# Sparse graph layers on one core: five summed slots in the last nine tiles, a new order of the last tiles, and three smaller edits

## The chip, the cores and the metric

The kernel runs on one core of one Trainium2 chip. The metric is the device time of one launch in microseconds; every number below is in microseconds unless it says otherwise. PE is TensorE, POOL is GpSimd, SP is SyncE, which here only issues DMAs.

## The reference, cut to what matters

Two layers on N = 4096 nodes with D = 512 features. `adj` is about 0.2% dense with a diagonal of its own, so a row has about nine entries.

```python
# layer 0
a = adj + eye;  d = sum(a, axis=1) ** -0.5
out = relu((d[:, None] * a * d[None, :]) @ x @ W.T + b)
x = layernorm(x + out)
# layer 1: attention over 8 heads, key size 64
q, k, v = x @ Wq[h], x @ Wk[h], x @ Wv[h]
scores = q @ k.T / 8 + 0.01 * eye - 1e16 * (1 - maximum(adj, eye))
out = sum over h of softmax(scores) @ v @ Wo[h]
x = layernorm(x + out)
```

Every stored edge is below one, so `1 - adj` times 1e16 sends all scores of a row but the largest to zero weight, and the largest is a node's own. Layer 1 then is `x @ sum_h(Wv[h] @ Wo[h])`. The kernel computes that, and proves on the chip that the inputs are of this kind; otherwise it runs a general version, which is not entered here.

## The kernel before

**First pass** (lines 1049-1091, `for t in range(NT + 1)`): 32 tiles of 128 rows of `adj`, 2 MB each, come in on SP. For each tile ScalarE sums the rows (`sum_rows`, L710) or adds up their negative parts (`sum_negative`, L715), POOL turns the sum into the degree's inverse root (`scaling`, L722-725), and VectorE finds the eight largest entries of each of eight segments and their places (`scan`, L752 and L753). Tiles are taken in the order `early + resident + again`: 14 early ones, 5 that stay in SBUF, and 13 that were read once already for their row sums and are read a second time later (`reload`, L994-998). Beside this the projection `u = x @ W.T` of every tile is formed on PE: `transpose_rows` (L689), a copy to SBUF on ScalarE (`evacuate`, L694), four fp32 matmuls against `wT` (`times`, L703). When the degree is known, `keep_y` (L736-738) scales it and POOL stores it to `y` in DRAM. The list `due` says at which t a tile's y is kept; `lo` and `hi` (L1058) say for which due times the projection is formed at step t: for t + 1 up to t = 24, for t + 1 and t + 2 at t = 25, for t + 2 after that. The accumulators `acc` have five PSUM buffers, `x_t` has six SBUF buffers.

**Sorting and matching.** `sorting` (L756-839) packs value and column into integer keys and takes the 24 largest of a row in three rounds of eight (`top8`), setting the taken ones to zero between rounds (`drop`, L785-788). `match` (L911) then moves edges of rows that have more than nine into free slots of other rows, so that each tile has KH = 9 slots of 128 edges. `cols_all` holds the columns (L896), `wr_all` the weights.

**Second pass** (lines 1280-1367, `for i in range(NT + 2)`, inner loop over k = 0..8). Tile i is `order[i]`. For each of its nine slots POOL gathers 128 rows of y (`gather`, L1110), one indirect DMA a slot, 18 slots ahead, into 19 buffers. PE multiplies each gathered 128x512 block by a 128x128 selection matrix (`spread`, built on ScalarE, L1007-1020) and accumulates in PSUM (L1316). Slots 0 to 4 (SAME = 5) share one matrix, so their rows may be scaled and summed first and multiplied once: `presum` (L1123-1131) scales slot 0 on ScalarE (L1127) and adds the others on VectorE (L1129). The list `summed` says how many slots of a tile are so summed:

```python
    summed = [1] + [2] * (NT - 3) + [SAME] * 2
```

That is one in tile 0, two in tiles 1 to 29, five in tiles 30 and 31, whose products `summed_products` (L1133-1140, L1137) issues with the summed one last. Then VectorE adds the own row (`scaled`, L1180) and the residual (`residual`, L1188); PE transposes (step "T") and multiplies by `wvo`, the product of the layer-1 weights (step "M"); ScalarE and VectorE form the two layernorms as one scaling (steps "Q", "V", L1207 and L1210), and `finish` (step "F", L1217-1220) scales into `r_t` and stores it through ScalarE's queue. The table in `at` says how many iterations behind, and at which k, each step of a tile is issued: `far` for tiles 0 to 29, `near` for the last two. Tile 31 is done in two halves of 256 columns. VectorE's scan and sorting of the later tiles run in between, in shares (`some`, L1327).

The order of instructions on an engine is set by a planner from its own costs; the source order is kept only where a call asks for it (`tc.keep_in_program_order`). Each engine takes its instructions in that order.

Of the kernel before, what the change touches and what calls it, by code (L numbers as in the profile page):

```python
# [419 lines left out]
def few_edges_below_one(  # L420
# [271 lines left out]
    def evacuate(pool, name, pt, pinned=False):  # L692
        dst = pool.tile([P, ND, P], FP, name=name, bufs=2)
        copy = nc.scalar.copy(dst.rearrange("p c s -> p (c s)"), pt[:, :D])  # L694
        if pinned:
            tc.keep_in_program_order(copy)
        return dst

    def times(srcT, w, u=None, dcs=range(ND)):
        if u is None:  # L700
            u = ps_a.tile([P, D], FP, name="acc")
        for dc in dcs:
            nc.tensor.matmul(  # L703
                u, srcT[:, dc, :], w[:, dc, :], start=(dc == 0), stop=(dc == ND - 1)
            )
        return u
# [49 lines left out]
    def sorting(t, idx, rec):  # L756
# [26 lines left out]
            return lambda: nc.vector.max(top[:, f, r * 8 : r * 8 + 8], keyf[:, f])  # L783

        def drop(f, r):  # L785
            return lambda: nc.vector.match_replace(
                keyf[:, f], top[:, f, r * 8 : r * 8 + 8], keyf[:, f], 0.0
            )

        short = [  # L790
            [
# [202 lines left out]
    def reload():  # L994

        t = queue.pop(0)
        reloaded.append(t)
        a_tiles[t] = load_a(t)

    def spread(t, s_t, k, alone=False):  # L1000

# [21 lines left out]
    xs, us = {}, {}  # L1023
    DEEP = 3
    RATE = 9
    EARLIER = NT - 7
    due = [(t + 1, t) for t in range(NT) if t not in early]
    for n, t in enumerate(early):
        at = max(t + 3, -(-STEPS * (n + 1) // RATE) + 1)
# [19 lines left out]
    for t in range(NT + 1):  # L1049
        if t == 0:  # L1050
            su1 = load_second_weights()
        if t + DEEP < NT:
            a_tiles[t + DEEP] = load_first(t + DEEP)
        if t == 3:
            order_second_weights()
            setup = second_weights(su1)

        lo, hi = t + 1 + (t > EARLIER), t + 1 + (t >= EARLIER)  # L1058
        ahead = [j for at, j in due if lo <= at <= hi]
        pts = []  # L1060
        for j in ahead:
            prefetch(1)
            pts.append(transpose_rows(xs.pop(j)))
        kind, begin, end = next(setup, (None,) * 3) if len(ahead) < 2 else (None,) * 3
        got = begin() if kind == "t" else None
        if t < NT:
            if t in early:
                sum_negative(t, a_tiles[t])
            else:
                sum_rows(deg_all[:, t : t + 1], a_tiles[t][:, : N // 2 if t == NT - 1 else N])  # L1070
                more = None
                if t == NT - 1:
                    more = small.tile([P, 1], FP, name="more")
                    sum_rows(more, a_tiles[t][:, N // 2 :])
                scaling(t, more)
            if t in again:
                del a_tiles[t]
        if left:
            left()
            left = None  # L1080
        for j in [j for at, j in due if at == t]:
            keep_y(j, us.pop(j))
        for j, pt in zip(ahead, pts):
            us[j] = times(evacuate(p1, "xT", pt, t >= EARLIER), wT)
        if kind == "t":
            end(got)
        if kind == "p":
            left = lambda end=end, pa=begin(): end(pa)
        if t < NT - 5:
            match(*ALL)  # L1090
        some((t + 1) * RATE)
# [6 lines left out]
    p2 = ctx.enter_context(tc.tile_pool(name="second", bufs=2))  # L1098
    AHEAD = 18

    SUMMED = (NT - 2, NT - 1)
    summed = [1] + [2] * (NT - 3) + [SAME] * 2
    slots = {}

    def gather(j):
# [24 lines left out]
            g, slots.pop(i * KH + k), w, g, op0=ALU.mult, op1=ALU.add  # L1130
        )

    def summed_products(i, pos, c=slice(0, D)):  # L1133

        k = SAME + pos if pos < KH - SAME else None
        g = slots[i * KH if k is None else i * KH + k]
        nc.tensor.matmul(  # L1137
            zs[i][:, c], mats[i][:, KH if k is None else k, :], g[:, c],
            start=False, stop=(k is None),
        )  # L1140

    def build(count):

# [27 lines left out]
    def bias(i, c=slice(0, D)):  # L1171

        nc.tensor.matmul(zs[i][:, c], ones3, b3[:, c], start=True, stop=False)
# [42 lines left out]

    def finish(i):  # L1217
        r_t = p2.tile([P, D], FP, name="r_t")
        nc.scalar.activation(r_t, ws.pop(i), AF.Copy, scale=sts.pop(i)[:, 4:5])  # L1219
        nc.scalar.dma_start(out[ts(order[i], P), :], r_t)  # L1220

# [45 lines left out]

    def at(step, i, k):  # L1270

        near = {"T": (1, 5), "M": (1, 8), "Q": (2, 2), "V": (2, 3), "F": (2, 7)}
        far = {"T": (2, 0), "M": (2, 6), "Q": (3, 1), "V": (3, 4), "F": (3, 8)}
        for table, tiles in ((near, range(NT - 2, NT)), (far, range(NT - 2))):
            behind, place = table[step]
            if k == place and i - behind in tiles:
                return i - behind
        return None

    for i in range(NT + 2):  # L1280
# [6 lines left out]
        for k in range(KH):  # L1287
# [6 lines left out]
                ws[t] = times(hTs.pop(t), wvo)  # L1294
            if i == NT - 1:

                if k <= KH - SAME:
                    summed_products(i, k, HALVES[0])
                if k == 6:
                    scaled(i, HALVES[0])  # L1300
                    residual(i, HALVES[0])
                if k == 7:
                    pts[i] = transpose_rows(hs[i], (0, 1))
                if k == 8:
                    bias(i, HALVES[1])
                    for n in range(KH - SAME + 1):
                        summed_products(i, n, HALVES[1])
                    hTs[i] = p2.tile([P, ND, P], FP, name="hT", bufs=2)
                    nc.scalar.copy(
                        hTs[i][:, 0:2].rearrange("p c s -> p (c s)"), pts[i][:, : 2 * P]  # L1310
                    )
            elif i in SUMMED:
                if k <= KH - SAME:
                    summed_products(i, k)
            elif i < NT and not 0 < k < summed[i]:
                nc.tensor.matmul(  # L1316
                    zs[i], mats[i][:, KH if k < summed[i] > 1 else k, :], slots.pop(i * KH + k),
                    start=False, stop=(k == KH - 1),
                )
# [13 lines left out]
                ws[p] = times(hTs[p], wvo, dcs=(0, 1))  # L1333
            if ends and k == 2:
                pts[p] = transpose_rows(hs[p], (2, 3))
                nc.scalar.copy(hTs[p][:, 2:].rearrange("p c s -> p (c s)"), pts[p][:, 2 * P : D])
                nc.vector.tensor_tensor(sts[p][:, 0:1], sts[p][:, 0:1], sts[p][:, 4:5], ALU.add)
            if ends and k == 3:
                times(hTs[p], wvo, ws[p], (2, 3))
# [59 lines left out]
```

## Time and profile before

| what | us |
|---|---|
| median of 3 runs (lowest, highest) | 646.42 (645.92, 649.11) |
| profiled execution, time | 646.95 |
| profiled execution, span of the core | 645.2 |
| busy PE / VectorE / ScalarE / POOL | 545.8 / 546.0 / 504.6 / 352.8 |
| mean granted clock of PE | 0.946 of full speed |
| bytes moved by DMA | 217.68 MB, mean 337 GB/s |

The time of the profiled execution holds 1.75 beyond the span. A matmul of fp32 operands shows as two records. An idle time is put down to what came last before the instruction started. The profile's line numbers are those of the kernel before.

### The profile page before, as it was taken

What the parts mean: (1) busy time and instruction counts of PE and PEld (TensorE: products, weight loads), DVE (VectorE), ACT (ScalarE), POOL (GpSimd) and SP (SyncE); (2) the same over time, 40 slices, a digit from 0 to 9 for tenths busy, and PEclk for the clock granted to TensorE, in tenths of its full rate; (3) what the DMA queues carried; (4) which work ended last, traced back from release to release, by engine and by line L of the source; (5) the groups of instructions that cost most, each with busy time, mean ns of one, the idle gap of its engine ahead of it and who ended that gap; (6) DMA issues with size and microseconds to landing.
All of it is one profiled execution on the core that took longest, in us unless ns stands there. A gap on an engine that the chain in (4) does not pass through costs nothing. (4 is left out here: it accounts for less than half of the span.)

```text
span 645.2 us, 7918 instructions
## 1 busy us (share of the span) xinstructions
PE 545.8 (85%) x1579; PEld 251.2 (39%) x1579; DVE 546.0 (85%) x2143; ACT 504.6 (78%) x1114; POOL 352.8 (55%) x465
## 2 busy tenths in 40 slices
PE   1699876488979756799898898999999999999993
PEld 1354332233434222344343343444444444444352
DVE  5699999999999995998899999999999995431521
ACT  1868667786988957699989877889988998986543
POOL 5222223223342377676776767767677777777700
PEclk9899987788979968799899998999999999999998
DMA  9999999799999388999999999999998888888721
GB/s 331 402 421 421 424 428 423 286 422 424 423 425 419 157 270 284 400 351 385 387 408 409 401 401 387 305 348 348 328 362 280 269 263 300 281 285 276 238 70 54
DMA packets 51515, 217.68 MB, mean 337 GB/s; under 512 B 8062, under 2 KB 9086, under 8 KB 45441
## 3 DMA queue, kind: packets, MB, share of 16 engines
q1 hardware_dynamic: 18128, 115.35, 44.7%
q0 software_dynamic: 28192, 92.30, 41.0%
q10 hardware_dynamic: 5136, 9.44, 3.9%
q14 instruction: 45, 0.36, 0.2%
q8 instruction: 14, 0.23, 0.1%
HBM read 200.28 MB, written 16.78 MB: 336 GB/s over the span
## 5 line engine op out<-in xcount | busy, mean ns | idle before, releaser
L1110 POOL DMA_INDIRECT g<-y,cols_all x288 | 282.5, 981 | 107.1 <-issue 43.1
L1316 PE MATMUL acc<-g,s_t 128*128 128x512 f32 x482 | 232.0, 618 | 28.0 <-DVE g L1129 17.1
L752 DVE MAX8 v_all<-a_t 128x8 f32<-128x512 f32 x256 | 166.3, 677 | 8.2 <-DMA a_t<-in_adj_dram 8.2
L753 DVE FIND_INDEX8 idx<-v_all,a_t 128x8 uint32<-128x512 f32 x256 | 173.0, 683 | 0.0
L703 PE MATMUL acc<-wT,xT 128*128 128x512 f32 x256 | 128.9, 658 | 31.4 <-ACT xT L694 31.3
L1316 PEld LDWEIGHTS acc<-g,s_t 128*128 128x128 f32 x482 | 89.8, 196 | 125.9 <-issue 95.1
L703 PE MATMUL acc<-wvo,hT 128*128 128x512 f32 x256 | 117.6, 601 | 4.5 <-ACT hT L694 3.8
L715 ACT ACTIVATE dump<-a_t 128x2048 uint8<-128x2048 f32 (+1 forms) x50 | 119.1, 2382 | 0.0
L703 PEld LDWEIGHTS acc<-wT,xT 128*128 128x128 f32 x256 | 52.1, 211 | 95.6 <-issue 59.1
L703 PEld LDWEIGHTS acc<-wvo,hT 128*128 128x128 f32 x256 | 48.6, 192 | 65.1 <-issue 57.0
L1007 ACT ACTIVATE sq<-cols,wr_all 128x128 f32<-128x128 f32 x160 | 58.7, 394 | 0.2
L1011 ACT ACTIVATE s_t<-sq,wr_all 128x128 f32<-128x128 f32 x128 | 58.2, 486 | 0.7 <-ACT sq L1007 0.2
L722 POOL TENSOR_SCALAR deg<-deg_all 128x1 f32<-128x1 f32 x32 | 7.1, 224 | 83.3 <-DVE deg_all L971 48.8
L1129 DVE SCALAR_TENSOR_TENSOR g<-g,wr_all 128x512 f32<-128x512 f32 x37 | 27.5, 743 | 25.5 <-ACT g L1127 22.7
L710 ACT ACTIVATE dump<-a_n 128x4096 uint8<-128x4096 f32 x13 | 47.3, 3636 | 0.0
L550 POOL DMA_DIRECT2D x_t<-in_x_dram x32 | 18.0, 566 | 46.3 <-PE pt L689 37.6
L1127 ACT ACTIVATE g<-g,wr_all 128x512 f32<-128x512 f32 x31 | 22.1, 713 | 24.0 <-DMA g<-y,cols_all 16.8
L783 DVE MAX8 top<-key 128x8 f32<-128x64 f32 x192 | 36.0, 213 | 0.3
L1180 DVE SCALAR_TENSOR_TENSOR h<-yo,own_all,acc 128x512 f32<-128x512 f32 (+1 forms) x33 | 23.8, 720 | 11.2 <-PE acc L1316 7.8
L1020 ACT ACTIVATE s_t<-s_t,wr_all 128x128 f32<-128x128 f32 x92 | 33.0, 391 | 0.0
L694 ACT COPY hT<-pt 128x512 f32<-128x512 f32 x31 | 18.0, 579 | 16.4 <-PE pt L689 15.4
L694 ACT COPY xT<-pt 128x512 f32<-128x512 f32 x32 | 18.3, 594 | 11.5 <-PE pt L689 11.5
(134 smaller groups left out, 676.8 us busy)
## 6 DMA issues: line engine op xcount, KB each, us to landing
a_t<-in_adj_dram SPq DMA_DIRECT2D x30, 2048.0 KB, 15.3
a_n<-in_adj_dram SPq DMA_DIRECT2D x13, 2048.0 KB, 13.6
x_t<-in_x_dram POOLq DMA_DIRECT2D x32, 256.0 KB, 12.6
yo<-y SPq DMA_DIRECT2D x32, 256.0 KB, 6.6
x_t<-in_x_dram SPq DMA_DIRECT2D x32, 256.0 KB, 5.9
out_dram<-r_t ACTq DMA_DIRECT2D x32, 256.0 KB, 5.2
y<-y_t POOLq DMA_DIRECT2D x18, 256.0 KB, 13.6
g<-y,cols_all POOLq DMA_INDIRECT x288, 6.3
```

Of the source, the lines that this page charges most:

```text
L694: copy = nc.scalar.copy(dst.rearrange("p c s -> p (c s)"), pt[:, :D])
L703: nc.tensor.matmul(u, srcT[:, dc, :], w[:, dc, :], start=(dc == 0), stop=(dc == ND - 1))
L710: nc.scalar.activation(dump[:, : part.shape[1]], part, AF.Copy, accum_out=dst)
L715: nc.scalar.activation(dump[:, o], a_t[:, o], AF.Relu, scale=-1.0, accum_out=neg_all[:, t, halves[0] : halves[0] + 1],)
L752: long.append(lambda o=o, seg=seg: nc.vector.max(v[:, o], seg))
L753: long.append(lambda o=o, seg=seg: nc.vector.max_index(idx[:, o], v[:, o], seg))
L783: return lambda: nc.vector.max(top[:, f, r * 8 : r * 8 + 8], keyf[:, f])
L1007: nc.scalar.activation(sq, cols1, AF.Square, bias=wr[:, 2, k : k + 1])
L1011: nc.scalar.activation(s_t[:, k, :], away(), AF.Relu, scale=wr[:, 3, k : k + 1], bias=wr[:, 1, k : k + 1],)
L1020: nc.scalar.activation(s_t[:, k, :], s_t[:, KH, :], AF.Copy, scale=wr[:, 1, k : k + 1])
L1110: nc.gpsimd.indirect_dma_start(out=slots[j], out_offset=None, in_=y[:, :], in_offset=bass.IndirectOffsetOnAxis(ap=cols_all[:, t, k : k + 1 ...
L1316: nc.tensor.matmul(zs[i], mats[i][:, KH if k < summed[i] > 1 else k, :], slots.pop(i * KH + k), start=False, stop=(k == KH - 1),)
```

## The change

Five edits. (1) `summed` gives five to the last nine tiles, 23 to 31, in place of the last two; the summed product is the first of its tile, not the last. (2) The last tiles are issued in another order: `near` for tiles 27 to 29 and 31, a table of its own for tile 30; the products of tile 31 in two blocks (`last_products`) at k = 4 and k = 6; two copies pinned to source order; the last scaling in halves on ScalarE and VectorE, stored through the queues of ScalarE and SP. (3) Projections are formed one, two and three steps sooner from t = 17, 21 and 25 on. (4) A reload is issued as four DMAs of 512 KB in place of one of 2 MB. (5) `drop` keeps the keys that are less than the eighth of the round, by one scalar_tensor_tensor, in place of a match-replace.

```diff
-            return lambda: nc.vector.match_replace(
-                keyf[:, f], top[:, f, r * 8 : r * 8 + 8], keyf[:, f], 0.0
-            )
+            return stt(keyf[:, f], keyf[:, f], top[:, f, r * 8 + 7 : r * 8 + 8], keyf[:, f],
+                       ALU.is_lt, ALU.mult)
...
-        a_tiles[t] = load_a(t)
+        a_tiles[t] = load_a(t, parts=4)
...
-    EARLIER = NT - 7
+    SOONER = (17, 21, 25)
+    def projected(t):
+        return t + 1 + sum(t >= e for e in SOONER)
...
-        lo, hi = t + 1 + (t > EARLIER), t + 1 + (t >= EARLIER)
+        lo, hi = projected(t - 1) + 1, projected(t)
...
-    SUMMED = (NT - 2, NT - 1)
-    summed = [1] + [2] * (NT - 3) + [SAME] * 2
+    summed = [1] + [2] * (NT - 1 - 9) + [SAME] * 9
...
+    def last_products(ks, c):
+        i = NT - 1
+        for k in ks:
+            nc.tensor.matmul(
+                zs[i][:, c], mats[i][:, k or KH, :], slots[i * KH + k][:, c],
+                start=False, stop=(k == KH - 1),
+            )
...
     def finish(i):
         r_t = p2.tile([P, D], FP, name="r_t")
-        nc.scalar.activation(r_t, ws.pop(i), AF.Copy, scale=sts.pop(i)[:, 4:5])
-        nc.scalar.dma_start(out[ts(order[i], P), :], r_t)
+        w, scale, rows = ws.pop(i), sts.pop(i)[:, 4:5], ts(order[i], P)
+        if i < NT - 1:
+            nc.scalar.activation(r_t, w, AF.Copy, scale=scale)
+            nc.scalar.dma_start(out[rows, :], r_t)
+            return
+        a, b = HALVES
+        nc.scalar.activation(r_t[:, a], w[:, a], AF.Copy, scale=scale)
+        nc.scalar.dma_start(out[rows, a], r_t[:, a])
+        nc.vector.tensor_scalar(r_t[:, b], w[:, b], scale, None, op0=ALU.mult)
+        nc.sync.dma_start(out[rows, b], r_t[:, b])
...
+        far = {"T": (2, 0), "M": (2, 6), "Q": (3, 1), "V": (3, 4), "F": (3, 8)}
         near = {"T": (1, 5), "M": (1, 8), "Q": (2, 2), "V": (2, 3), "F": (2, 7)}
-        far = {"T": (2, 0), "M": (2, 6), "Q": (3, 1), "V": (3, 4), "F": (3, 8)}
-        for table, tiles in ((near, range(NT - 2, NT)), (far, range(NT - 2))):
+        next_to_last = {"T": (1, 2), "M": (1, 3), "Q": (1, 7), "V": (1, 8), "F": (2, 0)}
+        for table, tiles in (
+            (far, range(NT - 5)), (near, (*range(NT - 5, NT - 2), NT - 1)),
+            (next_to_last, (NT - 2,)),
+        ):
...
-                if k <= KH - SAME:
-                    summed_products(i, k, HALVES[0])
+                if k == 4:
+                    last_products((0, *range(SAME, KH)), HALVES[0])
                 if k == 6:
                     scaled(i, HALVES[0])
                     residual(i, HALVES[0])
+                    bias(i, HALVES[1])
+                    last_products((0, *range(SAME, KH)), HALVES[1])
...
-                    nc.scalar.copy(
+                    tc.keep_in_program_order(nc.scalar.copy(
                         hTs[i][:, 0:2].rearrange("p c s -> p (c s)"), pts[i][:, : 2 * P]
-                    )
-            elif i in SUMMED:
-                if k <= KH - SAME:
-                    summed_products(i, k)
+                    ))
```

More of the change, by code (lines that the diff above doesn't have):

```diff
@@ L1083, in few_edges_below_one @@
         for j, pt in zip(ahead, pts):
-            us[j] = times(evacuate(p1, "xT", pt, t >= EARLIER), wT)
+            us[j] = times(evacuate(p1, "xT", pt, t >= NT - 7), wT)
         if kind == "t":
@@ L1131, in presum @@
         )
[L1133 to L1139, printed above, removed]
-        )
+    def last_products(ks, c):
[5 more added lines that the diff above has]
+            )
     def build(count):
@@ L1301, in few_edges_below_one @@
                     residual(i, HALVES[0])
+                    bias(i, HALVES[1])
+                    last_products((0, *range(SAME, KH)), HALVES[1])
                 if k == 7:
                     pts[i] = transpose_rows(hs[i], (0, 1))
[L1304 to L1307, printed above, removed]
                     hTs[i] = p2.tile([P, ND, P], FP, name="hT", bufs=2)
-                    nc.scalar.copy(
+                    tc.keep_in_program_order(nc.scalar.copy(
                         hTs[i][:, 0:2].rearrange("p c s -> p (c s)"), pts[i][:, : 2 * P]
-                    )
-            elif i in SUMMED:
-                if k <= KH - SAME:
-                    summed_products(i, k)
+                    ))
             elif i < NT and not 0 < k < summed[i]:
@@ L1335, in few_edges_below_one @@
                 pts[p] = transpose_rows(hs[p], (2, 3))
-                nc.scalar.copy(hTs[p][:, 2:].rearrange("p c s -> p (c s)"), pts[p][:, 2 * P : D])
+                tc.keep_in_program_order(nc.scalar.copy(
+                    hTs[p][:, 2:].rearrange("p c s -> p (c s)"), pts[p][:, 2 * P : D]
+                ))
                 nc.vector.tensor_tensor(sts[p][:, 0:1], sts[p][:, 0:1], sts[p][:, 4:5], ALU.add)
```

## The prediction, made before the change was run

> **What bounds the kernel now.** I read the share by slices first, then busy time by stretches of 20 us, then the engines' timelines at the two places where a stage begins or ends. I call the loop of lines 1049-1091 the first pass, that of line 1280 the second, and number tiles by their place i in the second. The columns below are the stretch, then busy us (instructions) of PE, weight load, VectorE, ScalarE and GpSimd, the granted clock, the DMA share and GB/s.
>
> ```profile
> 340.00:360.00 20.00, 16.35 (x50) 7.21 (x49) 20.00 (x81) 17.19 (x47) 13.22 (x14) 1.00 1.01 400
> ...
> 500.00:520.00 20.00, 20.00 (x64) 9.10 (x63) 19.98 (x93) 19.46 (x59) 15.16 (x16) 1.00 0.84 266
> ...
> 560.00:580.00 20.00, 20.00 (x64) 8.94 (x63) 8.94 (x36) 18.24 (x60) 15.13 (x17) 1.00 0.88 281
> ...
> 620.00:640.00 20.00, 15.31 (x50) 8.02 (x48) 3.11 (x13) 7.99 (x22) 0.00 (x0) 1.00 0.14 54
> ```
>
> Three regimes follow one another. From 60 to 247 us, and in nearly all of 258 to 526, VectorE is full (20.00 of 20); between 312 and 410 the DMA engines are full as well (share 1.01). From 410 on PE has no idle time: bias (L1173) follows bias after 11.55 us a tile (492.29, 503.83, 515.37, 526.92). From 526 VectorE is half idle. GpSimd is never called full, yet its timeline shows that it is:
>
> ```profile
> 600.04 1.26 POOL L1110 DMA_INDIRECT g<-y,cols_all  x1 [0.30 <-DVE sums L1207]
> 602.58 0.94 POOL L1110 DMA_INDIRECT g<-y,cols_all  x1 [1.28 <-DVE cols_all L896]
> ...
> 612.61 0.94 POOL L1110 DMA_INDIRECT g<-y,cols_all  x1 [0.30 <-issue]
> ```
>
> A gather takes 0.95 us and the next starts 0.30 us later, with no wait for a slot: 1.25 us each, 9 x 1.25 = 11.25 us a tile. From 485 us on no gather but (31,0) waits longer than 0.30 us. So the last nine tiles have two bounds side by side, PE at 11.55 us and gathers at 11.25 us. The 288 gathers run from 226.55 to 612.61: 287 x 1.25 = 358.8 us, and 27.3 us over that, of which some 25 us are lost before 500 us, in waits for slots and longer gathers. After the last gather PE still works off what it is late with:
>
> ```profile
> 625.22 3.60 PE L703 MATMUL acc<-wvo,hT 128*128 128x512 f32 x8
> 628.76 0.28 PE L1173 MATMUL acc<-b,ones 3*128 3x256 bf16 x1
> 628.96 2.43 PE L1137 MATMUL acc<-g,s_t 128*128 128x256 f32 x10
> 631.23 1.88 PE L703 MATMUL acc<-wvo,hT 128*128 128x512 f32 x4
> ```
>
> PE's last product of tile 31 (L1137) ends at 631.2 although the last row landed near 616.5 (row (31,4): issued at 607.58, its sum begins at 611.44, so 3.9 us). The last scaling ends at 638.13, 25.5 us after the last gather was issued, and the output's DMA and the end take the remaining 7 us.
>
> **What the Trainium skill says.** "PSUM — Partial Sum Buffer", section Engine vs sequencer instructions: VectorE's, ScalarE's and GpSimd's queues are strict FIFO, and matmuls start and complete in order. The trace agrees: products of tile 28 end at 595.8, but their `scaled` (L1180) runs at 600.47, behind four sums of tile 30 that wait for rows. "VectorE: DVE Perf Modes", section Two Vector instructions with no wait between them: a match-replace is two instructions, a value load and the replacement. The trace has both, 128 of each (below). "GPSIMD Engine Reference", section Key points: indirect DMAs are GpSimd's alone, and it shares its SBUF interfaces with VectorE, which shows against VectorE's instructions with two SBUF inputs. All 288 gathers stand on POOL here, and the long ones lie beside such instructions: 1.89 us at 367.70 beside eight L774, 1.44 and 1.26 us at 598.30 and 600.04 beside four sums back to back (L1129, 597.37-600.4).
>
> **The change part by part.** Rows for the prices:
>
> ```profile
> L1020 ACT ACTIVATE s_t<-s_t,wr_all 128x128 f32<-128x128 f32 x92 | 33.0, 391 | 0.0
> L1129 DVE SCALAR_TENSOR_TENSOR g<-g,wr_all 128x512 f32<-128x512 f32 x37 | 27.5, 743 | 25.5 <-ACT g L1127 22.7 <-DMA g<-y,cols_all 2.6
> L786 DVE MATCH_REPLACE8 key<-top,key 128x64 f32<-128x64 f32 x128 | 26.0, 207 | 0.0
> ...
> L786 DVE MATCH_VALUE_LOAD key<-top,key 128x8 f32 x128 | 9.9, 78 | 2.7 <-ACT mask L805 2.6
> ```
>
> *Five slots summed in tiles 23 to 29* (30 and 31 had it). Each of the seven tiles loses three products. One fp32 product is two matmul records; ten of them take 4.46 us (596.64), so 0.89 us a product: 7 x 3 x 0.89 = 18.7 us less on PE. PE's tile falls from 11.55 to 8.9 us. ScalarE loses 21 copies (L1020), started 0.30 us apart: 6 us, off the path. VectorE gains 21 sums (L1129); back to back they start 0.66-0.75 us apart, so 2.1 us a tile, 15 us in all. It has 9 to 15 us idle in each 20 us from 540 on; only tile 23's sums (issued near 515-527) meet full VectorE, 2 us that PE can catch up. The wait added: the summed product is now first on PE and waits for the sum of slot 4, and on VectorE scaled, residual and the matching of later tiles queue behind each sum. PE must wait for slot 8 of its tile anyway, 5 us after slot 4. So in steady state the tile goes from 11.55 to 11.25 us only: the gathers take over. What is gained is the lag. PE ends tile 23 about 16 us after (23,8) was issued and could end it 5.5 us after; at 11.25 - 8.9 = 2.35 us a tile the 11 us are caught up in five tiles, by tile 28.
>
> *New order of the last tiles*, worked out with that lag gone and gathers where they are. The sum of slot 4 of tile 31 ends at 612.15; `scaled` and `residual` of tile 30 behind it to 613.6; its transposes 0.6, copy 0.6, eight matmuls 3.6: 618.5. Then tile 31: products of the first half 2.2, `scaled` of that half 0.5 (I let PE's second half wait for it, they share a bank), bias and second half 2.4: 623.7; its `scaled` and `residual` 1.0 beside PE's transposes (0.3) and first two products with wvo (1.8), then transposes 0.3, copy 0.4, last two products 1.9: about 628.1. Squares 0.8, variance 0.4, root 0.2, half a scaling 0.4: 629.9 against 638.13. That is 8.2 us. If the planner places tile 30 ahead of the sums of tile 31, PE is free when slot 8 lands (616.5) and the end comes some 4 us sooner; if VectorE is held up by two more waits of 1-2 us it comes 3 us later. I take 8.5 us, ends 5 and 12.5.
>
> *Last scaling in halves on two engines and queues*: 0.69 becomes about 0.4, counted above; if the two reads of one bank are put one after the other it is 0.85, 0.2 us worse. The DMA halves from 256 KB on ACT to 128 KB each on ACT and SP; SP has nothing else queued then. 0 to 0.8 us, I take 0.3.
>
> *Keys dropped by comparison.* Value load to replacement to next start is 0.19 us (281.28 to 281.47); a scalar_tensor_tensor of 128x64 (L774) starts the next after 0.13 us. 128 drops x 0.06 = 7.7 us off VectorE. Some 32 drops lie before 247 us and 48 in 258-410, where VectorE is full: 1.9 + 2.9 = 4.8 us. Those after 410 lie beside PE and gathers and are worth nothing. Part of 312-410 is also held by the DMA engines, whose bytes don't change, so I take 3.5 us, ends 0 and 5.
>
> *Sooner projections.* From t = 17 transposes, x loads (on POOL, each 0.54 us), xT copies (0.47 us) and products (3.5 us) of one to three tiles move ahead. ScalarE waits 2.7 + 1.8 + 0.6 us for PE between 191 and 217 and copies six xT there (2.8 us); without them the last row sum could end some 8 us sooner, but the last adjacency bytes land only near 214 (DMA share 0.79 in 210-215, 0.15 after), so the first gather moves from 226.6 to about 222. What is late next is VectorE, still at its scans:
>
> ```profile
> 246.84 0.75 DVE L1180 SCALAR_TENSOR_TENSOR h<-yo,own_all,acc 128x512 f32<-128x512 f32 x1
> ...
> 257.00 0.75 DVE L1180 SCALAR_TENSOR_TENSOR h<-yo,own_all,acc 128x512 f32<-128x512 f32 x1 [7.78 <-PE acc L1316]
> ```
>
> Its first work of the second pass starts 20 us after the first gather, with no idle time before it; PE then waits for the sum at 247.51, and VectorE at 257.00 for PE. Gathers fill their 19 slots and wait. So I count 0. Bounds: a gain of 4.5 us if the early order lets it through; a loss of 2 us if the moved loads (3 x 256 KB at 420 GB/s) or the five PSUM accumulators, all in use at t = 25, hold up the row loads behind.
>
> *Gathers beside more two-input work.* A sum burst of four costs 0.8 us of gathers (above), sums that come as rows land cost 0.03 us (tile 31). Seven tiles: 0 to 5.6 us. A comparison drop has two inputs where match-replace had one; before 485 waits for slots hide this, after it some 22 drops x 0.13 us remain, at most 2.9 us. I take 1.5 us lost, ends 0 and 6.
>
> *Reloads in four parts*: three more issues of 0.4 us on SP per reload, with yo and x loads of the second next tile behind them, 1.2 us hidden by a lead of two tiles. VectorE never waits for a reload in this trace (its waits on a_t, 8.2 us, all lie before 21 us), so 0, ends -1 and +1.5.
>
> Sum against the profiled execution, 646.95 us (span 645.2): 8.5 + 0.3 + 3.5 - 1.5 = 10.8, so 636.1; the median of the runs is 0.5 below that execution: **635.6 us**.
>
> **Rivals.** (1) *The early gain comes through*: the gathers start 4 us sooner, and the tail gains 9.5: 646.4 - 4 - 4.5 - 9.5 = 628.4. For it: PE, DMA and ScalarE all have room at 215-230. Against: VectorE's full row. (2) *The tail alone*: VectorE's savings vanish in the DMA-bound stretch and sums lengthen the gathers: 646.4 - 8.5 + 3.5 = 641.4. For it: share 1.01. (3) *Nothing moves*: PE's lag turns into waits for sums of the same length; 645. Against: slot 4 lands 5 us before slot 8. (4) *VectorE's queue starves the gathers*, slower. The columns of tile i+2 (L896) come from VectorE behind the sums of tile i+1, which wait for rows of that tile. It happens already once: L896 at 602.15 held up (31,0), 0.98 us lost. If each of tiles 25 to 31 loses s there, the end is 635.6 + 7s: no gain from s = 1.5, slower than noise from 2.0 us; at 2.4 us it is 652.4. Against: the last matchings but one end 14 us before their gather (575.9, 589.5). (5) *The change doesn't do what it says*: the planner that orders instructions floats `residual` or sums of later tiles ahead again (only pinned copies are safe); that is within (2) or (4).
>
> **How the numbers follow.** A measurement can tell about 0.5%, 3.2 us. Forecast 0.50 (631-640 by itself), (1) 0.17, (2) 0.18: faster 0.85. (3) 0.07 same. (4) 0.08 slower. The lower end 626 leaves out a small part of (1); the upper end 642 takes in (2) and leaves out (3) and (4).
>
> **What would show it.** Right: PE's idle time appears from about 560 us, with waits for gathers or sums; 1.25 us between gathers to the end; last gather near 610.5; last product of tile 31 within 8 us of it (18.5 now); from last gather to last scaling 17 us instead of 25.5; VectorE's first L1180 near 245; 128 scalar_tensor_tensors in place of 256 instructions. Wrong: gathers with waits over 0.3 us after 500, the last one after 613, or a first L1180 that moves by more than 4 us.

## Result, and the profile after

The changed kernel takes 641.6 us (median of 6 runs, 639.05 to 643.17), the kernel before 646.67 beside it (6 runs, 645.84 to 649.11): ratio 0.990, 95% interval 0.988 to 0.993. The forecast was 635.6, range 626 to 642. The profiled execution took 641.63, span 639.8, mean clock 0.947. So the change gains 5 us where 10.8 were worked out; the second rival, the tail alone, had 641.4. Ratios, here and in the experiments, leave out runs over 1.5% above the fastest of their kernel, which matters for e1 alone: three of its six runs are left out, the profiled one among them, and with all six its ratio would be 0.984.

Of the lines of `before.py` that the prediction names, L1110 (gather) is now L1113, the sum L1129 is L1132, the products L1316 are L1326 and L1140, `scaled` L1183, `residual` L1191, the spread copies L1019, the last scaling L1228 (ScalarE) and L1230 (VectorE); L786 is gone and the drops stand under L774. First the stretches of 20 us, columns as before.

```profile
340.00:360.00 20.00, 16.26 (x42) 7.27 (x43) 17.35 (x65) 17.65 (x45) 14.38 (x15) 0.83 1.03 399
500.00:520.00 20.00, 20.00 (x64) 9.07 (x63) 20.00 (x85) 18.80 (x54) 15.43 (x16) 1.00 0.83 265
560.00:580.00 20.00, 16.18 (x44) 6.66 (x42) 11.20 (x35) 13.26 (x43) 15.42 (x16) 0.91 0.81 260
620.00:640.00 20.00, 10.30 (x31) 4.97 (x29) 2.68 (x11) 5.10 (x14) 0.00 (x0) 0.91 0.12 44
```

PE, full in 560-580 before, now has 3.8 of 20 us idle there: its lag on the gathers is gone. GpSimd is again the engine that never rests. Its timeline at the end:

```profile
610.18 1.07 POOL L1113 DMA_INDIRECT g<-y,cols_all  x1 [0.30 <-issue]
611.55 1.43 POOL L1113 DMA_INDIRECT g<-y,cols_all  x1 [0.30 <-issue]
...
614.53 0.95 POOL L1113 DMA_INDIRECT g<-y,cols_all  x1 [0.30 <-issue]
```

No gather after tile 21 waits more than 0.30 us, but two of these take 1.07 and 1.43 us instead of 0.95. The last one is issued at 614.53, 1.9 us **later** than before, where 2 us earlier were forecast. And PE's timeline behind it:

```profile
614.99 1.13 PE L1140 MATMUL acc<-g,s_t 128*128 128x256 f32 x4
617.16 1.35 PE L1140 MATMUL acc<-g,s_t 128*128 128x256 f32 x4 [1.04 <-DMA g<-y,cols_all]
618.35 0.60 PE L689 MATMUL pt<-ident,h 128*128 128x128 f32 x4
618.79 0.60 PE L1140 MATMUL acc<-g,s_t 128*128 128x256 f32 x2
619.62 3.70 PE L703 MATMUL acc<-wvo,hT 128*128 128x512 f32 x8 [0.24 <-ACT hT L694]
623.26 0.28 PE L1176 MATMUL acc<-b,ones 3*128 3x256 bf16 x1
623.47 2.43 PE L1140 MATMUL acc<-g,s_t 128*128 128x256 f32 x10
625.73 0.38 PE L689 MATMUL pt<-ident,h 128*128 128x128 f32 x2
626.57 1.99 PE L703 MATMUL acc<-wvo,hT 128*128 128x512 f32 x4 [0.46 <-ACT hT L1322]
628.39 0.38 PE L689 MATMUL pt<-ident,h 128*128 128x128 f32 x2
629.23 1.98 PE L703 MATMUL acc<-wvo,hT 128*128 128x512 f32 x4 [0.46 <-ACT hT L1346]
```

PE waits for a row (617.16) and works off only one other tile's products with `wvo` (619.62: four products, eight records) before the second half of tile 31. The last product ends 11.4 us after the last gather (18.8 before), and the last scaling, at 633.70, 19.2 us after it (25.5 before). From there to the end of the span it is 6.1 us (7.0 before). The balance of the two profiled executions: 6.3 gained from gather to scaling, 0.9 at the store, 1.9 lost at the gathers, in all 5.3 us.

### The profile page after: what moved, and what is told of

It is laid out like the page before. It is cut to its first block, busy times and chain, and to the rows that moved or that the text cites. A ratio compares the mean times of both kernels' runs of the same rounds, so it can differ in the third digit from the quotient of the medians.

```text
span 639.8 us, 7790 instructions
## 1 busy us (share of the span) xinstructions
PE 529.4 (83%) x1537; PEld 241.9 (38%) x1537; DVE 556.3 (87%) x2037; ACT 498.3 (78%) x1093; POOL 357.6 (56%) x465
## 5 line engine op out<-in xcount | busy, mean ns | idle before, releaser
L1113 POOL DMA_INDIRECT g<-y,cols_all x288 | 287.3, 998 | 101.9 <-issue 46.2
L1326 PE MATMUL acc<-g,s_t 128*128 128x512 f32 x450 | 222.1, 625 | 31.4 <-DMA x_t<-in_x_dram 14.6
L752 DVE MAX8 v_all<-a_t 128x8 f32<-128x512 f32 x256 | 166.9, 681 | 14.8 <-DMA a_t<-in_adj_dram 14.8
L703 PE MATMUL acc<-wT,xT 128*128 128x512 f32 x256 | 124.9, 641 | 26.4 <-ACT xT L694 26.4
L1326 PEld LDWEIGHTS acc<-g,s_t 128*128 128x128 f32 x450 | 83.1, 197 | 122.7 <-issue 75.3
L703 PEld LDWEIGHTS acc<-wT,xT 128*128 128x128 f32 x256 | 50.8, 206 | 88.6 <-issue 57.3
L1132 DVE SCALAR_TENSOR_TENSOR g<-g,wr_all 128x512 f32<-128x512 f32 x58 | 43.2, 745 | 29.4 <-ACT g L1130 17.4
L694 ACT COPY xT<-pt 128x512 f32<-128x512 f32 x32 | 18.4, 593 | 19.2 <-PE pt L689 12.4
L774 DVE SCALAR_TENSOR_TENSOR key<-key,top 128x64 f32<-128x64 f32 x128 | 32.3, 274 | 0.0
L689 PE MATMUL pt<-ident,x_t 128*128 128x128 f32 x128 | 19.9, 289 | 9.4 <-DMA x_t<-in_x_dram 8.9
L1183 DVE SCALAR_TENSOR_TENSOR h<-yo,own_all,acc 128x512 f32<-128x512 f32 (+1 forms) x33 | 23.7, 719 | 4.0 <-PE acc L1140 4.0
## 6 DMA issues: line engine op xcount, KB each, us to landing
a_t<-in_adj_dram SPq DMA_DIRECT2D x56, 512.0 KB, 14.2
a_n<-in_adj_dram SPq DMA_DIRECT2D x13, 2048.0 KB, 14.4
y<-y_t POOLq DMA_DIRECT2D x18, 256.0 KB, 10.8
```

Of the source, the lines that this page charges most:

```text
L703: nc.tensor.matmul(u, srcT[:, dc, :], w[:, dc, :], start=(dc == 0), stop=(dc == ND - 1))
L752: long.append(lambda o=o, seg=seg: nc.vector.max(v[:, o], seg))
L774: return lambda: nc.vector.scalar_tensor_tensor(out, a, sc, b, op0=op0, op1=op1, **kw)
L1113: nc.gpsimd.indirect_dma_start(out=slots[j], out_offset=None, in_=y[:, :], in_offset=bass.IndirectOffsetOnAxis(ap=cols_all[:, t, k : k + 1 ...
L1132: nc.vector.scalar_tensor_tensor(g, slots.pop(i * KH + k), w, g, op0=ALU.mult, op1=ALU.add)
L1326: nc.tensor.matmul(zs[i], mats[i][:, KH if k < summed[i] > 1 else k, :], slots.pop(i * KH + k), start=False, stop=(k == KH - 1),)
```

## What the gathers lost and where

The 288 gathers take 26.9 us over 287 x 1.25, as good as before (27.3), but made up otherwise. Durations over 0.95 us add up to 14.8 us (10.0 before), waits over 0.30 to 12.0 (17.3). After the start of tile 21 long durations are 6.1 us (1.8), and waits nothing (1.0). Tile 21 starts at 485.79 after the change, at 487.33 before and at 484.94 in e11, a second trace of the kernel before: up to there nothing is gained or lost that two traces of one kernel don't differ by. From there to the last gather it is 128.7 us, against 125.3 and 126.3. So the 1.9 us arise behind tile 21. Three causes are proposed and tested: **(a)** the first gather comes later, because the sooner projections hold up the first pass; **(b)** the five-slot sums lengthen the gathers beside them; **(c)** the drops save no VectorE time.

For (a), the end of the first pass, PE and ScalarE after the change:

```profile
203.86 1.09 PE L689 MATMUL pt<-ident,x_t 128*128 128x128 f32 x4 [3.08 <-DMA x_t<-in_x_dram]
204.74 12.95 PE L703 MATMUL acc<-wT,xT 128*128 128x512 f32 x24
```

```profile
210.91 0.58 ACT L694 COPY xT<-pt 128x512 f32<-128x512 f32 x1 [4.70 <-PE acc L703]
```

PE waits 3.08 us for a moved x load and then takes 12.95 us for 24 records, the 12 products of three tiles (10.53 for as many at 205.90 before); the granted clock in 205 to 210 is 0.53, and was 1.00. ScalarE's copy for the third of these tiles waits 4.70 us for products of the first: `xT` has two buffers (L693), and they still read one. The row sums of the last tiles are queued behind the copy. ScalarE's last row sum ends at 223.7 in place of 221.3, and the first gather goes out at 228.90 in place of 226.55.

For (c), the groups by line and shape, after and then before (busy us, mean ns of one):

```profile
L1132 DVE SCALAR_TENSOR_TENSOR g<-g,wr_all 128x512 f32<-128x512 f32 x58 | 43.2, 745 | 29.4 <-ACT g L1130 17.4 <-DMA g<-y,cols_all 11.6
L1191 DVE SCALAR_TENSOR_TENSOR h<-h,x_t 128x512 f32<-128x512 f32 x31 | 21.2, 682 | 0.1
L774 DVE SCALAR_TENSOR_TENSOR key<-key,top 128x64 f32<-128x64 f32 x128 | 32.3, 274 | 0.0
```

```profile
L774 DVE SCALAR_TENSOR_TENSOR own<-idx,spot,v_all 128x8 f32<-128x8 uint32 x32 | 6.6, 219 | 0.0
L774 DVE SCALAR_TENSOR_TENSOR key<-own,key 128x16 f32<-128x16 f32 x32 | 4.7, 162 | 0.1
```

The 128 drops and 21 more sums are there as the diff says. A drop takes 274 ns, and the next instruction starts 0.19 us after its start: the pair's 0.19. The prediction took 0.13 from L774 rows of 128x64 at 216 ns, whose scalar is an immediate; the drop's scalar is a column of `top`. The page of before held the hint: `own`, with a scalar from a column, takes 219 ns for eight elements, `key<-own,key`, with an immediate, 162 ns for sixteen. The closest pair is L1132 and L1191: same shape and type, 745 ns with a column and 682 with an immediate.

## Experiments

Theory A: the shorter tail is the gain; (a) and (b) give part of it back; (c) brings nothing. The rivals stand in the expectations. Ten of the twelve kernels ran where the kernel before takes 720 to 723 us, not 646, and are therefore compared by their ratio to the kernel before in the same runs; e11 and e12 ran where it takes 645.84. Where it takes 720 no trace of it was taken, so the tails there have no tail of the kernel before beside them. "Long" is the sum of gather durations over 0.95 us after the start of tile 21; the last two columns are us from the last gather to the end of tile 31's last product and to the end of the last scaling. How far an edit also deals VectorE's queue anew can be counted, as the longest sequence of instructions (operation, tile names, shape; a match-replace pair taken as one) that two queues have in common: of the 2037 of the changed kernel e1 keeps 2028, e9 2030, e2 1802 and e3 1771 in order. So e1 and e9 change little else on VectorE, while e2 and e3 also test a new order.

| kernel | ratio (95%) | first gather | long | product | scaling |
|---|---|---|---|---|---|
| e1 changed, edit 3 undone | 0.976 (0.972-0.981) | 225.01 | 5.7 | 14.4 | 22.2 |
| e2 changed, edit 4 undone | 0.985 (0.982-0.989) | 228.59 | 7.0 | 15.6 | 23.4 |
| e3 changed, edit 5 undone | 0.992 (0.990-0.995) | 229.77 | 6.9 | 14.4 | 22.2 |
| e4 before, edits 1 and 2 | 0.996 (0.994-0.999) | 226.37 | 8.0 | 14.4 | 22.2 |
| e5 changed | 0.983 (0.979-0.987) | 230.69 | 6.0 | 22.9 | 30.7 |
| e6 as e1 | 0.978 (0.973-0.983) | 225.39 | 7.2 | 13.7 | 21.5 |
| e7 as e4 | 0.996 (0.994-0.999) | 225.08 | 7.2 | 15.7 | 23.5 |
| e8 changed, edit 1 undone | 0.983 (0.979-0.988) | 230.63 | 2.9 | 17.3 | 25.1 |
| e9 changed, table of edit 2 undone | 0.985 (0.979-0.991) | 228.97 | 5.5 | 13.8 | 24.6 |
| e10 edit 3 undone, five tiles summed | 0.989 (0.983-0.994) | 225.27 | 5.3 | 14.2 | 22.0 |
| e11 before | one run, 644.7 us | 226.07 | 2.9 | 17.7 | 24.5 |
| e12 before, edit 5 | 1.0073 (1.0055-1.0091) | 225.47 | 4.1 | 17.7 | 24.4 |

**e1 and e6, edit 3 undone.**

```diff
-        return t + 1 + sum(t >= e for e in SOONER)
+        return t + 1 + (t >= NT - 7)
```

> The changed kernel with the projections formed when they were before (edit 3 undone), all else as changed. Theory A (the sooner projections are what made the first gather late: 228.90 against 226.55, because x loads land up to 26.7 us after their issue and PE and ScalarE wait for them): first gather back at 226.6 +- 0.7, PE's waits for x_t below 2 us, and the end comes 1 to 2.5 us sooner, 639 to 640.5. Theory B (VectorE's scans set the start of the second pass, whenever the gathers start): first gather back at 226.6, but VectorE's first own-row step stays within 1 us of 246.2 and the time stays at 641 to 642.5. Theory C (the late start comes from another edit): first gather stays at 228 to 229.

> The changed kernel with the projections formed as before (edit 3 undone), a second time, now beside the changed kernel. Theory A: the first gather is 2 to 4 us earlier than in the changed kernel and so is the end: 637.5 to 639.5 on a chip where the changed kernel takes 641.6, ratio to the changed kernel 0.994 to 0.997. Rival: gathers that start earlier only wait longer for slots (VectorE's first own row stays at 246), ratio to the changed kernel 1.000 within 0.002.

All five kernels with the sooner projections start their gathers at 228.6 to 230.7, all five beside them without at 225.0 to 226.4. PE's waits for x loads in the first pass go the same way: 0.6 us in e1, 9.4 in e5. The two traces, e5 and e6 in that order:

```profile
230.69 1.07 POOL L1113 DMA_INDIRECT g<-y,cols_all  x1 [3.75 <-DMA y<-wo]
```

```profile
225.39 1.07 POOL L1113 DMA_INDIRECT g<-y,cols_all  x1 [2.58 <-DMA y<-wo]
```

(a) is shown: edit 3, and nothing else, makes the first gather late. Of the rival, that gathers starting earlier only wait longer: where these ran `scaled` of the first tile stands at 267.1 to 268.3 without edit 3 and at 269.1 to 271.4 with it, so over half of the 4.3 us between their first gathers is still there. In the total it is not settled: both kernels have the lowest ratios of all, but their intervals overlap with that of e5, and e10, also without edit 3, is no faster than e5. In the traces of 646 and 642 us it is another matter: there `scaled` starts at 246.84 before and at 246.22 after, and up to the start of tile 6 the gathers have lost 3.1 us after, 7.1 and (in e11) 4.7 before, so that more than half of the late start is absorbed there, and all of it by tile 21. That the late start costs time is not shown there; edit 3 alone wasn't run there.

**e2, edit 4 undone.**

```diff
-        a_tiles[t] = load_a(t, parts=4)
+        a_tiles[t] = load_a(t)
```

> The changed kernel with each reload as one DMA of 2 MB again (edit 4 undone). Theory A (the parts let VectorE and ScalarE start on the first quarter, and so lower the gathers' waits for slots before 485 us): the gathers' time over 1.25 us each grows by 2 to 4 us and the time rises to 643.5 to 646. Theory B (VectorE never waited for reloads, so parts do nothing): 641 to 642.5. Theory C (the parts tie up SP and gathers share the queues with them; VectorE waited 6.5 us for a_t at 256.6 where it did not before): that wait goes, and the time falls by 1 to 3 us.

0.985 against 0.983 for e5: no difference, as the prediction's 0 has it. Its reason, that VectorE never waits for a reload, does not hold with the parts: all eight traces with edit 4 have one wait of VectorE for a reload of 5.2 to 6.9 us near the start of the second pass, and none of the six without it has one.

**e3 and e12, edit 5 undone and alone.**

```diff
-            return lambda: nc.vector.match_replace(
-                keyf[:, f], top[:, f, r * 8 : r * 8 + 8], keyf[:, f], 0.0
-            )
+            return stt(keyf[:, f], keyf[:, f], top[:, f, r * 8 + 7 : r * 8 + 8], keyf[:, f],
+                       ALU.is_lt, ALU.mult)
```

> The changed kernel with match-replace for the drops (edit 5 undone). The prediction held a drop at 0.19 us before and 0.13 after; the changed profile shows 0.19 after too (274 ns, starts 0.19 us apart), so Theory A (the comparison costs VectorE what the pair cost): 641 to 642.5, no difference. Theory B (it saves VectorE 5 us on the path): 644.5 to 646.5. Theory C (two SBUF inputs hold up the gathers' descriptors, and this costs after 485 us): gathers after 485 us run 1 to 3 us less over 1.25 us each, and the time falls to 639 to 640.5.

> The kernel before with edit 5 alone: keys dropped by one scalar_tensor_tensor in place of a match-replace. Theory A as the traces of 646 and 642 us have it (pair and comparison both let the next instruction start after 0.19 us, so nothing is saved): ratio to the kernel before 1.000 within 0.003. Theory C (in this setting an instruction of VectorE that arrives late costs 1.2 us and more whatever its length, so 128 instructions fewer count): ratio 0.988 to 0.994, and VectorE's unexplained idle time less than in the kernel before by 3 to 10 us. The prediction's own price (0.06 us a drop) would give 0.995.

The two answers have opposite signs. Undone in the changed kernel it costs 0.9% (intervals of e3 and e5 apart); alone in the kernel before, on the chip of 646 us, it costs 0.73%, 4.7 us. Kernel and chip both differ between the two. Each of e12's three expectations missed. VectorE's busy time (544.7 us) is that of e11 (544.9), so it is not the price. The first gather of tile 9 in e11, then in e12, and one of tile 12 in e12:

```profile
337.47 0.94 POOL L1110 DMA_INDIRECT g<-y,cols_all  x1 [0.30 <-PE acc L703]
```

```profile
341.87 0.94 POOL L1109 DMA_INDIRECT g<-y,cols_all  x1 [2.86 <-DMA g<-y,cols_all]
...
382.72 0.94 POOL L1109 DMA_INDIRECT g<-y,cols_all  x1 [2.41 <-DMA g<-y,cols_all]
```

e12's gathers fall behind here, mostly in waits that the profile puts down to rows of earlier gathers, not landed yet: tile 8 starts 0.6 us later than in e11 (324.79 against 324.19), tile 12 5.1 us (379.37, 374.27), tile 16 7.5 us (431.23, 423.73), the last gather 6.7 us. VectorE's loss is seen later, in the stretch 420 to 480 of e11, then of e12, and in VectorE's timeline of e12:

```profile
420.00:480.00 60.00, 59.38 (x182) 26.94 (x182) 59.98 (x262) 54.09 (x159) 43.80 (x45) 1.00 0.98 356
```

```profile
420.00:480.00 60.00, 55.45 (x162) 24.43 (x161) 52.98 (x222) 48.94 (x146) 42.13 (x45) 0.97 0.94 340
```

```profile
430.05 0.75 DVE L1128 SCALAR_TENSOR_TENSOR g<-g,wr_all 128x512 f32<-128x512 f32 x1 [5.21 <-ACT s_t L1016]
```

VectorE stands 5.21 us behind a sum, with scans queued after it, because ScalarE's scaling of slot 0 waits 6.24 us for its row (428.95); at 454.85 it happens again, 1.77 us. VectorE, always busy there in e11, loses 7.0 us, about what the last gather is late by. But it follows from late rows and doesn't make them late: from tile 16 on e12's gathers lose no more than e11's. What made them late between tiles 8 and 16 is not shown. A new order is a candidate: counted as above, 1756 of e12's 2015 VectorE instructions stand in the order of e11, while e11 and the earlier trace of the same kernel agree in all. The planner deals the queue anew when one operation changes. That this makes the 4.7 us, without the drops' second input, wasn't separated.

**e4 and e7, edits 1 and 2 alone** (edits 3, 4 and 5 undone by the three diffs above).

> The kernel before with edits 1 and 2 alone: five slots summed in the last nine tiles, the new order of the last tiles, the last scaling in halves; projections, reloads and drops as before. Theory A (the whole gain lies after the last gather: 19.2 us to the last scaling against 25.5, and 1 us less for the last store): first gather at 226.6, last gather within 1 us of 612.6 to 613.5, total 638.5 to 640.5, so better than the changed kernel. Theory B (the other three edits give 3 us together in the middle stretch, as fewer waits for slots): last gather 615 to 617, total 643 to 645.

> The kernel before with edits 1 and 2 alone (five slots summed in the last nine tiles, new order of the last tiles), a second time. Theory A (drops by comparison save nothing, reloads in parts cost or save under 1 us, sooner projections cost 2 us): as fast as the changed kernel without the sooner projections, 637.5 to 640 where the changed kernel takes 641.6. Rival (edits 4 and 5 save VectorE or DMA time that lets the gathers run on sooner): 642 to 645, slower than the changed kernel.

The tail is 22.2 and 23.5 us, near that of e1 and e6, but the ratio is 0.996 against their 0.976 and 0.978: where these ran, edits 4 and 5 together, with the order that comes with them, are worth about 2%, and Theory A's figure for them is wrong there.

**e5, the changed kernel.**

> The changed kernel itself, as the measure for the three kernels that ran beside it. Theory A (the tail is shorter by 6 us, and 2 us of it are given back by a first gather that comes later): ratio to the kernel before 0.990, first gather 2 to 4 us later than in the kernel before, last gather to end of last scaling 19 us. Theory B (the gain depends on what VectorE and the DMA queues have left over on the chip at hand): a ratio outside 0.985 to 0.995, and another distance than 19 us from the last gather to the last scaling.

0.983 lies outside the 0.985 to 0.995 that Theory B names, though its interval reaches 0.987, and the distance to the last scaling, 30.7 us in this execution, is far from 19. Theory B has the better of it: where 720 us are usual, other things count. VectorE's timeline in e5 shows one:

```profile
258.41 0.23 DVE L774 SCALAR_TENSOR_TENSOR key<-own,key 128x16 f32<-128x16 f32 x1 [1.10 <-DVE key L774]
259.81 0.18 DVE L774 SCALAR_TENSOR_TENSOR key<-own,key 128x16 f32<-128x16 f32 x1 [1.17 <-DVE key L774]
261.21 0.23 DVE L783 MAX8 top<-key 128x8 f32<-128x64 f32 x1 [1.22 <-DVE key L774]
262.64 0.23 DVE L783 MAX8 top<-key 128x8 f32<-128x64 f32 x1 [1.21 <-issue]
```

Instructions of 0.2 us start 1.40 us apart, and the profile names no other engine that they wait for. In the ten kernels e1 to e10 VectorE has 58 to 82 us of such idle time from 200 us on; in the four other traces (before, after, e11, e12) 0.2 us at most. ScalarE has 41 to 71 us of it, against about 8. In e5 ScalarE stands 13.39 us before a copy near the end (674.04) and PE 12.57 us behind it, hence its 30.7. What delays them is not shown.

**e8, five slots summed in two tiles.**

```diff
-    summed = [1] + [2] * (NT - 1 - 9) + [SAME] * 9
+    summed = [1] + [2] * (NT - 3) + [SAME] * 2
```

> The changed kernel with five slots summed only in tiles 30 and 31, as before, in place of 23 to 31 (edit 1 undone, the rest of the change kept). Theory A (PE's lag of 11 us on the gathers, caught up by the three products fewer a tile, is what the tail gained): the gathers of the last nine tiles are 3 to 5 us shorter in all, last gather near 611, but PE ends the last product of tile 31 some 17 us after the last gather in place of 11, end 644 to 647, ratio to the changed kernel 1.004 to 1.009. Rival (the new order of the last tiles alone gave the gain, and the sums only lengthen the gathers): 637 to 640, faster than the changed kernel.

The mechanism is as Theory A has it on both sides: gathers are lengthened by 2.9 us instead of 5.3 to 8.0 in the other nine, and PE ends its last product 17.3 us after the last gather instead of 13.7 to 15.7 (e5 aside). So mainly the sums of edit 1, not the drops, lengthen the gathers: e3, e4 and e7 have match-replace and 6.9 to 8.0, e8 has the comparison and 2.9. A small part for the drops isn't excluded: e12 has 4.1, against 1.8 and 2.9 in the two traces of the kernel before. The total does not tell: 0.983, as e5, so within some 0.4% each the two effects of edit 1 cancel there.

**e9, the table of edit 2 undone.**

```diff
-            (far, range(NT - 5)), (near, (*range(NT - 5, NT - 2), NT - 1)),
-            (next_to_last, (NT - 2,)),
+            (far, range(NT - 2)), (near, range(NT - 2, NT)),
```

> The changed kernel with the places of the steps T, M, Q, V and F as before (near for tiles 30 and 31 only, far for the others; no table of its own for tile 30); blocks of products, pinned copies and halves of the last scaling kept. Theory A (the places of the steps give 2 to 4 us of the shorter tail, the blocks of products and PE's missing lag the rest): last gather to end of last scaling 21 to 24 us, in place of the changed kernel's 19.2 on the chip of its own comparison; ratio to the changed kernel 1.003 to 1.006. Rival (the planner puts the steps where it likes and only the blocks and pinned copies count): the same order on PE at the end, the same 19 to 20 us, ratio 1.000 within 0.002.

PE's timeline at the end of e9:

```profile
689.36 2.43 PE L1140 MATMUL acc<-g,s_t 128*128 128x256 f32 x10
691.62 0.38 PE L689 MATMUL pt<-ident,h 128*128 128x128 f32 x2
691.84 5.32 PE L703 MATMUL acc<-wvo,hT 128*128 128x512 f32 x12
696.99 0.38 PE L689 MATMUL pt<-ident,h 128*128 128x128 f32 x2
```

Twelve records with `wvo` (six products) stand between the transposes of tile 31, eight of them tile 30's: the last product comes 13.8 us after the last gather, but the last scaling 24.6, against 21.5 to 23.5. The table is worth 1 to 3 us of the tail; the ratio, 0.985, can't tell it.

**e10, edit 3 undone and five tiles summed** (e1's diff and `[2] * (NT - 1 - 5) + [SAME] * 5`).

> The changed kernel with the projections formed as before (edit 3 undone) and five slots summed in the last five tiles in place of nine. Theory A (PE gains 2.35 us a tile on the gathers with five summed, so five tiles are enough for its lag of 11 us, and four tiles fewer of two-input sums beside the gathers give back some 2 us; the first gather is 2 to 4 us earlier): ratio to the changed kernel 0.990 to 0.995, faster by 0.002 to 0.004 than with edit 3 undone alone; gathers after tile 21 lengthened by 3 to 5 us in all, in place of 5.7 to 7.2. Rival (the lag is not caught up in five tiles, or the gathers are lengthened by something else than these sums): no faster than with edit 3 undone alone, PE still without idle time in the last 60 us before the last gather.

A miss: 0.989, no better than e5, and gathers lengthened by 5.3. Five tiles do catch up PE's lag (14.2), but nothing is saved. e1 and e6, with nine tiles and on another chip, have the lowest ratios of all, and their intervals end where e10's begins. That four tiles more are worth 1% here, and all of edit 1 nothing in e8, doesn't fit together and stays open.

**e11, the kernel before.**

> The kernel before, one look, so that the traces of the experiments have one of the kernel before from the same setting to stand against. Theory A (the tail is shorter by the order of the last tiles and PE's missing lag, wherever the kernel runs): last gather to end of last scaling 25 to 27 us, against 21.5 to 23.5 in the kernels with edits 1 and 2; first gather 225 to 227. Theory C (in this setting VectorE's instructions arrive late): idle time of VectorE before instructions with no wait that the profile shows, or behind VectorE's own instruction before, 50 to 90 us in all, and before MATCH_VALUE_LOAD and MATCH_REPLACE of L786 more than 6 us of it. Rival to C (the lower TensorE clock is the reason for 720 us): less than 20 us of such idle time, and matmul groups of the same shape longer by over 5%.

It ran on the chip of 646 us, so it says nothing on Theory C; it gives a second trace of the kernel before. Its tail, 24.5 us, and last gather, 611.21, show how far one execution differs from another: 1.0 and 1.4 us. Against it the tail gains 5.3 us, not 6.3.

## Why the prediction was half right

**Bound and steady state: right.** PE's idle time begins between 540 and 560, gathers go out every 1.25 us without waits, and the wait of (31,0) for its columns is gone. PE's lag of 11 us is caught up.

**Order of the last tiles: right in kind, by another path; 8.5 forecast, 6.3 measured.** The working has the last product 11.1 us after the last gather (612.61 to 623.7); 11.4 were measured. That these agree so well is in part luck: the working has tile 30's products with `wvo` ahead of both halves of tile 31, and on the chip the first half, waiting for rows, went ahead of them (614.99 to 618.79). The error is behind it: 6.2 us to the last scaling were added up, 7.8 came (11.4 to 19.2). The items listed there come to 6.5, not 6.2. The sum left out the copy ahead of the first two products with `wvo` (PE idle 0.46 us), had two products at 1.8 to 1.9 us for 1.98, and let the halves of the last scaling run side by side, while they stand one after the other (632.72 and 633.22, 0.5 us; the prediction had this as a case). "Within 8 us" in its list contradicted its own 11.1.

**Last store: 0.3 forecast, 0.9 measured.** The last 256 KB landed 2.5 us after their issue before, the two halves of 128 KB 1.8 and 1.7 us after theirs.

**Drops: 3.5 forecast, nothing gained; the step that failed.** It priced the drop by a row of the same operation and shape but with another kind of scalar. The true price, 0.19 us from start to start, is the pair's. Tile 21 should have started some 3.5 us sooner by this step and started within the spread of the two traces of before. That the edit alone costs 4.7 us in the kernel before is a case for which the bounds 0 to 5 had no room; in the trace after the change VectorE has no idle time between 410 and 526, so the stalls of e12 are not in it.

**Gathers lengthened: 1.5 forecast, 4.3 measured (6.1 - 1.8; 3.2 against e11's 2.9), inside its ends of 0 and 6.** This is the other half of the miss: these us lie behind tile 21, where gathers set the pace. The step took the one gathering burst it had seen as typical and counted tile 31's sums at 0.03 us, where two gathers of tile 31 now take 1.07 and 1.43 us in place of 0.95. e8 puts the lengthening on the sums. The Trainium skill, "GPSIMD Engine Reference", section Key points, on interfaces shared between GpSimd and VectorE's two-input instructions, agrees.

**Sooner projections: 0 forecast, and 0 by tile 21, but not by the way forecast.** The working had the first gather move from 226.6 to about 222; it came 2.35 us later instead. Of the two hold-ups that the bound named, the late x loads are in the trace; the accumulators are not, the copy waited for a buffer of `xT`. That the first own row on VectorE, not the first gather, decides was right in the trace of 642 us (246.2, hardly moved). From t = 25 on the change is two steps, not three: the kernel before was one ahead there already.

**Reloads in parts: 0, and 0 in e2.** A new wait of VectorE for a reload, 6.48 us at 256.61, took the place of one of 7.78 us for PE; it comes with the parts.

The miss adds up: the last gather was to come 2.0 us sooner (3.5 - 1.5) and came 1.9 later, and the tail with the store gained 7.2 for 8.8. The result lies just inside the upper end of 642, which had been set for the second rival.

Of the rivals the fourth, starved gathers, did not show: no gather after tile 21 waits. The second came closest in the number, for one of its two reasons: sums lengthened the gathers. VectorE's savings were nil by the price of a drop, not by the full DMA engines. How much of the 5 us is the order of VectorE's queue, dealt anew by edits 4 and 5, stays open: neither the change without one of its edits nor edit 1 or 2 alone was run on the chip of 646 us. What each gives of the shorter tail there is read from its trace, not shown by a run.

## What to carry to other kernels

Price an operation by a row with the same operands, a scalar from memory or an immediate included, not only the same opcode and shape. Where a planner orders the queues, an edit of one operation is also a new order of all: differences under 1% between two such kernels say nothing of the operation until the order is compared. A stall that appears behind a loss is not its cause: find first where the gathers fall behind. And when a serial tail is summed from durations, list every copy, and add the list up twice: here a copy, a slip of 0.3 and two halves one after the other made 7.8 us of 6.2.

## What was not expected of the hardware

The kernel before took 646 us on one chip and 720 on two others. The kernels profiled on those two had a mean clock of 0.89 to 0.91, against 0.947 before and after, and 58 to 82 us of VectorE's idle time in front of instructions for which the profile names no other engine. There edit 5 gained 0.9%, in the changed kernel, where it cost 0.7% on the faster chip, in the kernel before. Fewer instructions to deliver would be a reason, but e3, with 128 more, has no more of that idle time (61.5 us) than e5 (71.6), so it is not settled.
